# First attention of a two-layer kernel: the eight products of a unit in one block, and the values, turns and unloads after them

## The chip, the cores and the metric

The kernel runs on one NeuronCore of a Trainium2 chip. The metric is the device time of one execution in microseconds (us), lower is better. PE is the matrix engine (TensorE), DVE the vector engine, ACT the scalar engine, POOL the GpSimd engine, SP the queue that issues most DMAs. PSUM is the memory that PE writes into; a "bank" below is one PSUM buffer of 128 partitions by 512 floats, and the kernel has eight of them.

## The reference, cut to what matters

Four batches of 1,024 tokens with 256 features go through two layers: attention, feed-forward, attention, and a mixture of experts, each with a residual and a layer norm. All is float32. The change touches the first attention, which has 16 heads of 16 dimensions:

```python
qkv = jnp.einsum('bsc,oc->bso', x, w_qkv).reshape(B, S, 3, H, D)
q = layer_norm(qkv[:, :, 0], q_gamma, q_beta)
k = layer_norm(qkv[:, :, 1], k_gamma, k_beta)
v = qkv[:, :, 2]
q, k = apply_rope(q, k)
attn = jnp.einsum('bqhd,bkhd->bhqk', q * D ** (-0.5), k)
attn = jax.nn.softmax(attn, axis=-1)
out = jnp.einsum('bhqk,bkhd->bqhd', attn, v).reshape(B, S, C)
out = jnp.einsum('bsc,oc->bso', out, w_proj) + b_proj
```

## The kernel before, in words

**Groups and units.** The 16 heads of a batch are worked on in four groups of four heads, so there are sixteen groups in all, numbered n = 4b + g. Each group goes over its 8 x 2 blocks of scores (128 by 512) twice. The first pass (class `Maxima`, `head`, line 467) makes the scores with queries on the partitions, and DVE reduces each to its row maxima (line 470). The second pass (class `Attend`, `head`, line 491) makes the scores again with keys on the partitions and the maximum folded in as a seventeenth dimension, and ACT takes the exponential (line 500). `values` (line 509) then multiplies the exponentials with the values. Both products have only up to 32 rows to contract over, and each of the four heads lies in its own 32 partitions, so they are "row-tile" products: four of them can run in the array at once. The value products write 32 partitions each and are "column-tile" products. Everything else on PE (projections, transposes, feed-forward) uses the whole array.

**The unit.** `first_units(b)` (from line 1047) runs the second pass of group n together with the first pass of group n+1. For each of 16 steps i it puts out a unit: four score products of group n (`at.head`), four of group n+1 (`mx.head`), and the values of step i-1. A float32 product is two rows of the profile, so the eight products are sixteen rows. Before the change they stand in two blocks of four products. The values stand between the two blocks, and so does, in some steps, one of these: a `turn` (line 458: four transposes that make queries or keys feature-major, copied out by ACT, line 461; at i = 3, 10 and 12 to 15) or an `unload` (line 524: four transposes of the attention's output, read out by DVE, lines 527 and 528; at i = 5 for the last group, and at i = 11). The last group of the last batch has no group after it, so its units hold only four products.

**Banks.** The score products of both kinds take their banks in turn from one pool of six (`ps_s`, tag `s`). The values have one bank of their own (`ps_av`), and turns, unloads and all pieces of other work inside these units share the last one (`ps_m`, tag `m`, asked for with `bank(name, False)`, line 139). A product can start when the reader of the bank's last tile is done.

**What sets the order.** All this runs inside a hand-written schedule: the order in which the Python code puts instructions out is the order on each engine's queue. `weave` (line 1139) takes unit after unit and puts pieces of other stages (projections, feed-forward, routing) between them, about as many as there are units or fewer. At PE the queue is thus: block, values, turn or unload, block, piece, next unit. Work due later (`later`, `tick`) goes on DVE and POOL between units.

Of the kernel before, what the change touches and what calls it, by code (L numbers as in the profile page):

```python
# [35 lines left out]
def postln_layers_kernel(ctx: ExitStack, tc: tile.TileContext, a: dict, out: bass.AP):  # L36
# [74 lines left out]
    with ExitStack() as main:  # L111
# [932 lines left out]
        groups = {}  # L1044
        oq0, oT1, ends = {}, {}, {}

        def first_units(b):

            oq0[b] = act.tile([P, TB, C], F32, tag="oq", bufs=2, name=f"oq0_{b}")
            last = None  # L1050
            for g in range(G0):
                n = 4 * b + g
                at = Attend(groups[n], oq0[b])
                mx = groups.get(n + 1)
                for i in range(16):
                    for hp in range(2):

                        then = []
                        for j in range(2):
                            if mx is not None:  # L1060
                                then += [at.head(i, 2 * hp + j), mx.head(i, 2 * (1 - hp) + j)]
                            elif hp == 0:
                                then += [at.head(i, 2 * j), at.head(i, 2 * j + 1)]
                        for fn in then:
                            fn()
                        if hp == 0:
                            if i > 0:
                                at.values(i - 1)
                            elif last is not None:
                                last.values(15)  # L1070
                            if i == 3:
                                groups[n].turn(0, 1, name="a")
                            if i == 5 and last is not None:
                                last.unload(1)
                            if i == 10 and mx is not None:
                                mx.turn(0, 0, name="a")
                            if i == 11:
                                at.unload(0)
                            if i >= 12 and n + 2 in groups:
                                groups[n + 2].turn((i - 12) // 2, i % 2)  # L1080
                    if i == 0:
                        groups[n].close(1)
                    if i == 3 and n + 2 < G0 * B:
                        nb, ng = divmod(n + 2, G0)
                        groups[n + 2] = Maxima(nb, ng)
                    if i >= 4 and n + 2 in groups:
                        groups[n + 2].rotate(4)
                    if i == 8 and mx is not None:
                        mx.close(0)
                    yield  # L1090
                last = at
            last.values(15)

            def end(big):
                last.unload(1, big)

            ends[b] = end
# [206 lines left out]
        def second_end(b):  # L1304
# [4 lines left out]
        cut = 19  # L1309
        weave(  # L1310
            first_units(0), 64, early + stash, False, [lambda big: load_heads(1, 0)], 30, [f for f in prep if f], 0
        )
        flush()
        load_ahead()
        load_heads(1, 1)
        for t in range(TB):
            load_x(1, t)
        weave(first_units(1), 64, project_v(1) + first_end(0) + ffn0(0) + project1(0), False, [lambda big: load_heads(2, 0)], 30)
        for b in (1, 2):
            ffn = ffn0(b)  # L1320
            ends_b = first_end(b)
            weave(
                second_units(b - 1),
                29,
                ends_b[:1] + load_v(b + 1) + [lambda big, b=b: load_heads(b + 1, 1)] + ends_b[1:] + ffn[:cut],
                True,
            )
            weave(
                first_units(b + 1),
                64,  # L1330
                second_end(b - 1) + ffn[cut:] + project1(b),
                False,
                [lambda big, b=b: load_heads(b + 2, 0)] if b + 2 < B else (),
                30,
                dispatch(b - 1, False),
                30,
            )
# [261 lines left out]
```

## Time and profile before

| what | value |
|---|---|
| three runs | 2453.25, 2458.11, 2460.34 us; median 2458.11 us |
| the profiled execution | 2456.11 us |
| its span, first to last instruction | 2454.4 us (1.7 us lie around it) |
| mean granted PE clock | 0.958 |
| stretches with units of the first attention | 71.8 to 703.0, 864.5 to 1186.3, 1349.1 to 1647.9 us |
| granted clock from 71.8 to 364.2, 364.2 to 703.0, 864.5 to 1186.3, 1349.1 to 1589.6 us | 1.00, 1.00, 0.99, 1.00 |
| PE, DVE, ACT, POOL busy in the span | 2317.0, 1385.0, 1018.4, 741.7 us |

The page of the profile counts an engine's busy time, then follows the chain of work that ended last back through the span. The groups add up all instructions of one line. The timeline lists single instructions in order of time; `xN` at a line's end means that N of them were merged, and square brackets give the engine's idle time before the instruction and what ended it. The ends of matmuls in it are modelled, so that rows of PE overlap and a PE that waits for less than the pipeline's length still counts as busy. What a step of PE costs is therefore read from start to start: from its first row to the first row of the next step. `32*128` means that a product contracts over 32 rows (row tile), `128*32` that it writes 32 columns (column tile), `128*128` the whole array.

### The profile page before, as it was taken

How to read it: one execution, taken by the hardware profiler on the slowest of the kernel's cores; microseconds unless marked ns; L12 is line 12 of the kernel's file. 1: busy time of each engine (PE TensorE's matmuls, PEld its weight loads, DVE VectorE, ACT ScalarE, POOL GpSimd, SP SyncE). 2: the span in 40 equal slices, each digit the busy share in tenths (PEclk: the TensorE clock that was granted, in tenths of full speed). 3: DMA queues.
4: the chain of work that ended last, by engine and by line, in shares of the span. 5: the costliest groups of instructions: out<-in, count | busy, mean ns of one | idle time of the engine just before them, and what ended most of it. 6: DMA issues, size and time to landing. Idle time of an engine off the chain costs nothing.

```text
span 2454.4 us, 36158 instructions
## 1 busy us (share of the span) xinstructions
PE 2317.0 (94%) x14004; PEld 1150.6 (47%) x14004; DVE 1385.0 (56%) x3227; ACT 1018.4 (41%) x2037; POOL 741.7 (30%) x1101
## 2 busy tenths in 40 slices
PE   8999999999999999999999999999999974999994
PEld 5333334444444543444445434445566432666662
DVE  7766666666557376785573867716635673111113
ACT  2565655555543445545333554562332231111112
POOL 5335337223214144262241420301111153222223
PEclk9999999999989999999899999998999786999997
DMA  3233120000000000010000000111000011444444
GB/s 102 61 128 132 55 78 29 18 11 1 1 28 1 1 1 23 1 65 15 32 1 1 1 1 10 61 44 57 1 1 1 1 66 57 112 112 106 105 88 148
DMA packets 78124, 107.77 MB, mean 44 GB/s; under 512 B 8832, under 2 KB 67200, under 8 KB 76288
## 3 DMA queue, kind: packets, MB, share of 16 engines
q1 hardware_dynamic: 48592, 73.34, 9.1%
q0 software_dynamic: 9984, 14.82, 3.2%
q10 hardware_dynamic: 19376, 17.30, 2.3%
q8 instruction: 110, 1.80, 0.3%
q14 instruction: 62, 0.51, 0.1%
HBM read 66.54 MB, written 38.90 MB: 43 GB/s over the span
## 4 chain that ended last, share of the span: by engine, by line
PE 87%; DVE 8%; DMA 1%; POOL 1%; issue 1%; ACT 1%; SPq 0%; DVEq 0%; POOLq 0%; ACTq 0%
PE sc L491 20%; PE av L509 10%; PE ph L1460 7%; PE gu L655 7%; PE py L1476 7%; PE sc L981 5%; PE mx L931 4%; PE mx L467 4%; PE p L900 4%; PE dn L671 4%; PE av L1018 3%; PE dn L1018 2%; DVE masked L941 2%; PE ppa L589 2%; PE qk L320 2%; PE pt L458 1%
## 5 line engine op out<-in xcount | busy, mean ns | idle before, releaser
L470 DVE TENSOR_REDUCE part<-mx 128x1 f32<-128x512 f32 x1024 | 655.9, 684 | 304.9 <-PE mx L467 299.3
L500 ACT ACTIVATE pe<-sc 128x512 f32<-128x512 f32 x1024 | 554.1, 596 | 397.3 <-PE mx L467 344.3
L467 PE MATMUL mx<-kT,qT 32*128 32x512 f32 x2048 | 630.5, 638 | 2.1 <-DVE part L470 1.9
L491 PE MATMUL sc<-qT,kT 32*128 32x512 f32 x2048 | 605.6, 638 | 0.0
L491 PEld LDWEIGHTS sc<-qT,kT 32*128 32x128 f32 x2048 | 176.4, 183 | 219.5 <-issue 175.8
L509 PE MATMUL av<-pe,va 128*32 128x512 f32 x2048 | 273.8, 606 | 0.0
L992 ACT ACTIVATE pe<-sc 128x512 f32<-128x512 f32 (+3 forms) x384 | 157.3, 498 | 215.6 <-PE sc L981 215.3
L467 PEld LDWEIGHTS mx<-kT,qT 32*128 32x128 f32 x2048 | 189.2, 183 | 40.2 <-DVE part L470 21.2
L941 DVE CUSTOM_DVE_ANT_0 masked<-mx,mask_w 128x128 bf16<-128x128 f32 (+3 forms) x256 | 125.5, 490 | 121.2 <-PE mx L931 89.5
L1460 PE MATMUL ph<-dmT,f 128*128 128x512 f32 x384 | 170.2, 602 | 4.4 <-DVE dmT L99 3.5
L1468 ACT ACTIVATE hTm<-ph,b 128x512 f32<-128x512 f32 x96 | 60.7, 683 | 261.3 <-PE ph L1460 261.3
L1476 PE MATMUL py<-f,hTm 128*128 128x256 f32 x768 | 167.7, 379 | 0.0
L995 POOL TENSOR_SCALAR_AFFINE_SELECT pe<-pe 128x256 f32<-128x256 f32 x128 | 53.8, 429 | 369.6 <-ACT pe L992 368.0
L1480 POOL DMA_INDIRECT acc_d<-yo,dm x48 | 74.7, 1555 | 285.1 <-DVE yo L1478 243.6
L1476 PEld LDWEIGHTS py<-f,hTm 128*128 128x128 f32 x768 | 146.2, 190 | 24.7 <-issue 5.7
L931 PE MATMUL mx<-kT,qT 32*128 32x512 f32 (+3 forms) x768 | 144.0, 603 | 4.1 <-DVE x L556 3.2
L385 POOL TENSOR_TENSOR ss<-ss,neg_half 128x16 f32<-128x16 f32 x48 | 139.1, 2906 | 0.5
L1477 DVE TENSOR_TENSOR yo<-py,b 128x256 f32<-128x256 f32 x48 | 20.4, 425 | 207.2 <-PE py L1476 207.2
L981 PE MATMUL sc<-qT,kT 32*128 32x512 f32 (+3 forms) x768 | 131.7, 577 | 3.6 <-DVE part L941 2.0
L509 PEld LDWEIGHTS av<-pe,va 128*32 128x32 f32 x2048 | 40.5, 108 | 192.4 <-issue 186.2
L1460 PEld LDWEIGHTS ph<-dmT,f 128*128 128x128 f32 x384 | 72.9, 192 | 94.7 <-issue 86.6
L655 PE MATMUL gu<-xTf,wg 128*128 128x256 f32 x384 | 107.3, 402 | 0.3 <-ACT pe L992 0.3
(346 smaller groups left out, 2955.6 us busy)
## 6 DMA issues: line engine op xcount, KB each, us to landing
f<-in_fc SPq DMA_DIRECT2D x14, 1024.0 KB, 5.0
f<-in_fc ACTq DMA_DIRECT2D x10, 1024.0 KB, 6.3
disp_d<-empty ACTq DMA_DIRECT2D x12, 520.0 KB, 3.4
xink<-in_xT SPq DMA_DIRECT2D x24, 256.0 KB, 2.9
qk_d<-xs SPq DMA_DIRECT2D x6, 1024.0 KB, 5.1
xr<-qk_d SPq DMA_DIRECT2D x6, 1024.0 KB, 7.1
dm<-disp_d SPq DMA_DIRECT2D x11, 520.0 KB, 3.7
x<-in_x SPq DMA_DIRECT2D x32, 128.0 KB, 2.8
```

The source lines that it names most:

```text
L467: nc.tensor.matmul(sc, self.qT[r, t * P : (t + 1) * P], self.kT[r, u * 512 : (u + 1) * 512], start=True, stop=True)
L470: return lambda: nc.vector.tensor_reduce(self.part[:, t, u, h : h + 1], sc, AX.X, ALU.max, negate=True)
L491: nc.tensor.matmul(sc, self.m.kT[r, kt * P : (kt + 1) * P], self.m.qT[r, qb * 512 : (qb + 1) * 512], start=True, stop=True)
L500: nc.scalar.activation(self.pes[i, h // 2][:, h % 2, :], sc, AF.Exp)
L509: nc.tensor.matmul(self.av[32 * h : 32 * h + 32, :], va0[:, kt, 4 * self.g + h, :], self.pes[i, h // 2][:, h % 2, :], start=kt == 0, stop= ...
L655: nc.tensor.matmul(ps[:, i * 256 : (i + 1) * 256], w[:, c, f * P : (f + 1) * P], xT[j][:, c, :], start=c == 0, stop=c == 1,)
L931: nc.tensor.matmul(scs[h][:, :n], qT[r, t * P : (t + 1) * P], kT[r, u * 512 : u * 512 + n], start=True, stop=True,)
L941: nc.vector.tensor_tensor_reduce(masked[:, :n], scs[h][:, :n], mask_w[:, 512 - n :], -1.0, -NEG, ALU.add, ALU.min, part)
L981: nc.tensor.matmul(scs[h][:, off:], ones_h[r, :] if w else kT[r, kt * P : (kt + 1) * P], (self.m.nmT if w else qT)[r, q], start=w == 0, st ...
L992: nc.scalar.activation(pe[:, j, off:], scs[2 * hp + j][:, off:], AF.Exp)
L1460: nc.tensor.matmul(ph[:, i * CAP : (i + 1) * CAP], f1[:, c, (f + i) * P : (f + i + 1) * P], dmT[:, c, :], start=c == 0, stop=c == 1,)
L1476: nc.tensor.matmul(py[:, :C], hT[:, f, c * P : (c + 1) * P], f2[:, f, :], start=f == 0, stop=f == FF1 // P - 1)
```

## The change

Inside a unit the loop over two halves (`hp`) is gone. The four heads' products of both groups are put out one after the other, eight products in one block; behind them come the values of the step before, and then the turn or unload of the step. The pairs of heads stay the same (`at` head h with `mx` head h+2 modulo 4), and so does the order of products, exponentials and maxima. Number, shape and buffers of all instructions stay the same. On PE the queue of a unit becomes: block of eight, values, turn or unload, piece. On ACT the copy of a turn stands behind four exponentials, where it stood behind two; on DVE the two reads of an unload stand behind four maxima, where they stood behind two. POOL and SP keep their order. In the last group, which has no `mx`, the order of instructions stays as it was.

```diff
                 for i in range(16):
-                    for hp in range(2):
-
-                        then = []
-                        for j in range(2):
-                            if mx is not None:
-                                then += [at.head(i, 2 * hp + j), mx.head(i, 2 * (1 - hp) + j)]
-                            elif hp == 0:
-                                then += [at.head(i, 2 * j), at.head(i, 2 * j + 1)]
+
+                    for h in range(4):
+                        then = [at.head(i, h)]
+                        if mx is not None:
+                            then.append(mx.head(i, (h + 2) % 4))
                         for fn in then:
                             fn()
-                        if hp == 0:
-                            if i > 0:
-                                at.values(i - 1)
-                            elif last is not None:
-                                last.values(15)
-                            if i == 3:
-                                groups[n].turn(0, 1, name="a")
-                            if i == 5 and last is not None:
-                                last.unload(1)
-                            if i == 10 and mx is not None:
-                                mx.turn(0, 0, name="a")
-                            if i == 11:
-                                at.unload(0)
-                            if i >= 12 and n + 2 in groups:
-                                groups[n + 2].turn((i - 12) // 2, i % 2)
+                    if i > 0:
+                        at.values(i - 1)
+                    elif last is not None:
+                        last.values(15)
+                    if i == 3:
+                        groups[n].turn(0, 1, name="a")
+                    if i == 5 and last is not None:
+                        last.unload(1)
+                    if i == 10 and mx is not None:
+                        mx.turn(0, 0, name="a")
+                    if i == 11:
+                        at.unload(0)
+                    if i >= 12 and n + 2 in groups:
+                        groups[n + 2].turn((i - 12) // 2, i % 2)
```

## The prediction

> **What bounds the kernel now.** I read the page first, for the bound, then the timeline of PE through the units of the first attention, then the two places in it where the trace already shows what the change makes of every unit.
>
> ```profile
> PE 2317.0 (94%) x14004; PEld 1150.6 (47%) x14004; DVE 1385.0 (56%) x3227; ACT 1018.4 (41%) x2037; POOL 741.7 (30%) x1101
> ...
> PE 87%; DVE 8%; DMA 1%; POOL 1%; issue 1%; ACT 1%; SPq 0%; DVEq 0%; POOLq 0%; ACTq 0%
> ...
> L470 DVE TENSOR_REDUCE part<-mx 128x1 f32<-128x512 f32 x1024 | 655.9, 684 | 304.9 <-PE mx L467 299.3
> L500 ACT ACTIVATE pe<-sc 128x512 f32<-128x512 f32 x1024 | 554.1, 596 | 397.3 <-PE mx L467 344.3
> ```
>
> PE carries the chain (87%). The two readers of the score banks wait for PE and not the other way round: DVE idles 304.9 us before its maxima, ACT 397.3 us before its exponentials. So time on PE in these units is time of the kernel. An ordinary unit with a piece (PE rows of the timeline; one row of each step left in, each block has eight):
>
> ```profile
> 447.38 0.69 PE L491 MATMUL sc<-qT,kT 32*128 32x512 f32 x1
> ...
> 447.91 0.59 PE L491 MATMUL sc<-qT,kT 32*128 32x512 f32 x1
> ...
> 448.45 1.07 PE L509 MATMUL av<-pe,va 128*32 128x512 f32 x8
> 449.44 0.69 PE L491 MATMUL sc<-qT,kT 32*128 32x512 f32 x1
> ...
> 450.51 1.13 PE L655 MATMUL gu<-xTf,wg 128*128 128x256 f32 x4
> ...
> 452.44 0.69 PE L491 MATMUL sc<-qT,kT 32*128 32x512 f32 x1
> ```
>
> From start to start: block 1.07 us, values 0.99, block 1.07, piece 1.93. No gap: PE sets the pace. The second block costs no wait although it needs two banks that the first one filled (eight products, six banks): the values give ACT and DVE 0.99 us to empty them.
>
> **What sixteen rows in one block cost.** Where no piece stands between two units, the second block of one and the first of the next already touch. The trace has 47 such long blocks: 46 of 3.00 to 3.01 us and one of 4.93. One of the 46 (rows of PE, ACT and DVE, in order of time):
>
> ```profile
> 280.86 0.69 PE L491 MATMUL sc<-qT,kT 32*128 32x512 f32 x1
> ...
> 282.02 1.57 ACT L500 ACTIVATE pe<-sc 128x512 f32<-128x512 f32 x3 [0.47 <-PE mx L467]
> 282.06 1.29 DVE L470 TENSOR_REDUCE part<-mx 128x1 f32<-128x512 f32 x2 [1.36 <-PE mx L467]
> ...
> 282.26 1.10 PE L491 MATMUL sc<-qT,kT 32*128 32x512 f32 x2
> 282.81 0.69 PE L467 MATMUL mx<-kT,qT 32*128 32x512 f32 x1
> ...
> 283.86 1.07 PE L509 MATMUL av<-pe,va 128*32 128x512 f32 x8
> ```
>
> The first four products run together; the next two take the last free banks; the seventh and eighth cannot start before the first exponential and the first maximum, which begin at 1.16 and 1.20 us, are done. They start at 1.87 and 1.95 us (282.81 is the eighth) and the block ends at 3.00. Apart from each other, two blocks cost 2 x 1.07 = 2.14. So one block of sixteen rows costs 3.00 - 2.14 = **+0.86 us**.
>
> A rule of the Trainium skill speaks for the change: "TensorEngine Tiling (Array Packing)", section Tiling Modes, says that changing the tiling mode drains the engine, and the change makes each unit change mode less often. The rows bear the drain out: at the edges of a block a pass of four takes 0.53 us, and inside the long block the second pass gives way after 0.43 (0.53 to 0.96). By the drain alone one long block would take 4 x 0.43 + 2 x 0.10 = 1.92 us and save 0.22 in a unit, 190 x 0.22 = 42 us in all (the 190 comes below). By the row it takes 3.00, this saving already in it. The row decides, because it holds the bank wait too.
>
> **The change part by part.** I went through PE's timeline unit by unit. 240 of the 256 units have eight products; the last 16 have four and keep their order, cost nothing.
>
> *Units without a piece* cost nothing: their 3.00 us seam between units is taken away and put inside a unit, with the values now at the seam. *Units with a piece*: 52, 62, 45 and 31 in batches 0 to 3, together 190 (a unit that had no values between its blocks, at the start of a batch, is left out). There 2.14 becomes 3.00: 190 x 0.86 = **+163 us**. Nothing covers it; the values that covered it now come after the wait.
>
> Corrections of that, from the same timeline. Where the piece is a gate and up product (48 units), DVE's two operations on it let the maxima start 1.32 us after the block's start (448.70 against 447.38) rather than 1.20, which the values hid: 48 x 0.12 = +6. In about 28 units DVE's or another engine's work delays the second block already, to 1.8 us or more; there the delay stays, the values no longer lie in it, and the cost is a whole 1.00 rather than 0.86: 28 x 0.14 = +4. In 23 units that follow a short piece (0.59 us of transposes) the first block takes 1.34, not 1.07, since it waits for the banks of the block just before; the values will stand in between: 23 x 0.27 = -6. Together **+4 us**.
>
> *Turns and unloads move* from between the blocks to just ahead of the piece. They write the bank `m`, and so does every piece in these units; with the one bank, the piece has to wait for the copy out. Before, the second block (1.07 us) lay in between and hid this. The last group, with no second block, shows it uncovered, a turn first, then an unload (PE, ACT and DVE rows):
>
> ```profile
> 1598.31 0.66 PE L458 MATMUL pt_1a<-ident,tokq 128*128 128x128 f32 x4
> 1599.38 0.62 ACT L461 COPY qT<-pt_1a 128x512 f32<-128x512 f32 x1
> 1600.06 1.13 PE L900 MATMUL p<-xTa,w1q 128*128 128x256 f32 x4 [1.09 <-ACT qT L461]
> ...
> 1606.38 0.66 PE L524 MATMUL pto<-ident,avs 128*128 128x128 f32 x4
> 1607.08 0.26 DVE L527 RECIPROCAL rc<-pto 128x16 f32<-128x16 f32 x1 [19.96 <-PE pto L524]
> 1607.37 0.42 DVE L528 TENSOR_TENSOR oq<-pto,rc 128x256 f32<-128x256 f32 x1
> ```
>
> The unload's piece starts at 1607.94, 1.56 us after the unload; the four transposes themselves take 0.59, so the wait is 0.97. DVE is free then as it will be after the change: the fourth maximum ends near 3.0 + 0.1 + 0.7 = 3.8 us of a unit, the unload at 3.00 + 1.00 + 0.59 = 4.59. The turn's copy begins late in this row because ACT still has exponentials (1.07 us). After the change they end near 3.6, a full microsecond before the turn does, so I take the delay of a turn with a free ACT: in the unit at 280.27 the copy begins 0.70 after the transposes (280.97), takes 0.58, and 0.06 more pass before the piece as in the row above: 1.34 - 0.59 = 0.75. Bounds: 0 if something hid it, 1.16 if ACT were as late as in the row shown (1.75 - 0.59). 92 of the 190 units have both a turn or unload and a piece: 69 turns x 0.75 = 52 and 23 unloads x 0.97 = 22, **+74 us**. A turn without a piece behind it is followed by a long block, which needs other banks, and costs nothing.
>
> What queues behind the new waits: behind the seventh product on PE stand the eighth, the values and the piece; ACT and DVE get the last two tiles later, but wait for PE anyway. The exponentials are needed by the values of the next unit only, after its long block. The later copy of a turn is first read in the next unit or later. POOL's and SP's queues keep their order, and longer units only give their transfers more room: nothing, or a few us less of the present waits.
>
> Sum: 163 + 4 + 74 = +241 us, on the profiled execution's 2456.1 (span 2454.4 and 1.7 around it): 2697. The median of the runs shown is 2.0 above that execution, so I say **2698 us**.
>
> **The rivals.**
> - *Only the bank wait*: if the copy of a turn or unload were hidden after all, 163 + 4 remain: 2625. The rows of the last group speak against it. 8%.
> - *A deeper backlog*: the wait for the first maximum passes every delay of DVE on to PE, with no values to absorb it; if this cost 0.25 us more in each of the 190 units, +48: 2746. Against it: 46 equal long blocks in the trace, in busy and quiet stretches. 8%.
> - *The drain counts and the banks don't*: a long block of 1.92 and the turn's waits, 2456 - 42 + 74 = 2488. Against it: those same 46. 2%.
> - *Not slower: emptying the banks is the bound already.* If four maxima and the work of a piece on DVE (4 x 0.64 + 0.84 = 3.4 us in the unit shown) set the unit's length, a wait on PE would lie inside it and the time would stay at 2458. It decides from the point where DVE's work exceeds PE's 5.06 us of that unit; it is 1.66 short, and DVE's 304.9 us of idling say the same. 2%.
>
> The forecast has 80%.
>
> **How the numbers follow.** Its own range: the long block between +0.83 and +1.00 in 190 units (158 to 190), the turns and unloads between 0.55 and 0.98 in 92 (51 to 90): 2456 + 209 to 2456 + 280, 2665 to 2736. I give 2655 to 2738, which reaches some way towards both slower-side rivals. Faster by over 0.3% (about what a measurement of this kernel can tell from no change): 1%; within it 2%; slower 97%.
>
> **What would show it.** In the profile after, PE's timeline should show blocks of sixteen rows of 3.0 us in nearly all 240 units, their last two products starting near 1.9 us; the wait of `mx` (L467) for `part` (L470) and of `sc` (L491) for `pe` (L500) should grow, by number more than by the idle time, as the modelled ends hide part of it. Pieces behind a turn should wait for `qT` or `kT` (L461), those behind an unload for `oq` (L528). A long block near 1.9 us would break the first step; pieces that start 0.59 us after a turn, the second. Second attention and experts should stay as long as they are.

## The result and the profile after

The changed kernel takes 2676.91 us (median of four runs, 2674.09 to 2679.78) against 2457.73 us before: a ratio of 1.091, 95% interval 1.088 to 1.095. The forecast was 2698 us, in a range of 2655 to 2738.

The page of the kernel after, lines of parts 1, 4 and 5:

```profile
PE 2479.7 (93%) x14004; PEld 1234.3 (46%) x14004; DVE 1386.5 (52%) x3227; ACT 1025.9 (38%) x2037; POOL 742.3 (28%) x1101
...
PE 87%; DVE 7%; ACT 2%; issue 1%; POOL 1%; DMA 1%; SPq 0%; DVEq 0%; POOLq 0%; ACTq 0%
...
L470 DVE TENSOR_REDUCE part<-mx 128x1 f32<-128x512 f32 x1024 | 656.3, 684 | 351.2 <-PE mx L467 346.8
L500 ACT ACTIVATE pe<-sc 128x512 f32<-128x512 f32 x1024 | 554.2, 598 | 343.7 <-PE mx L467 282.9
```

This page alone would mislead. PE does the same 14,004 rows and is "busy" 163 us longer: most of the new waiting lies inside the modelled length of matmuls and counts as work. The share of 93% says nothing about PE being well used. ACT has 2% of the chain now, where it had 1%: of its 60 us there, 43 are the copies of line 461 that pieces wait for. The waits show only from start to start. One unit with a gate and up piece after the change, from the timeline (PE, ACT and DVE; the unit is of the same kind as the one shown of before):

```profile
526.07 0.69 PE L491 MATMUL sc<-qT,kT 32*128 32x512 f32 x1
...
527.23 1.57 ACT L500 ACTIVATE pe<-sc 128x512 f32<-128x512 f32 x3 [0.67 <-PE mx L467]
527.39 2.58 DVE L470 TENSOR_REDUCE part<-mx 128x1 f32<-128x512 f32 x4
...
528.12 0.69 PE L467 MATMUL mx<-kT,qT 32*128 32x512 f32 x1
...
529.17 1.07 PE L509 MATMUL av<-pe,va 128*32 128x512 f32 x8
530.17 1.13 PE L655 MATMUL gu<-xTf,wg 128*128 128x256 f32 x4
...
532.09 0.69 PE L491 MATMUL sc<-qT,kT 32*128 32x512 f32 x1
```

The block lasts 3.10 us (529.17 - 526.07). Its eighth product starts at 528.12, 0.73 after DVE began the first maximum at 527.39. The four maxima take 2.58, so the first is done near 528.03, just before that product starts: its bank is what the product waits for. The unit takes 6.02 us where it took 5.06. Of the 240 units with eight products, 160 have a block of exactly 3.00, 49 one of 3.10 to 3.12 (48 units have a gate and up piece).

A turn and an unload, each with its piece, from the same timeline:

```profile
141.77 0.66 PE L458 MATMUL pt<-ident,tokq 128*128 128x128 f32 x4
142.47 0.59 ACT L461 COPY qT<-pt 128x512 f32<-128x512 f32 x1 [1.06 <-PE pt L458]
143.10 1.13 PE L320 MATMUL qk<-w,xink 128*128 128x256 f32 x4 [0.68 <-ACT qT L461]
...
186.47 0.66 PE L524 MATMUL pto<-ident,avs 128*128 128x128 f32 x4
187.17 0.26 DVE L527 RECIPROCAL rc<-pto 128x16 f32<-128x16 f32 x1 [0.89 <-PE pto L524]
...
188.03 1.10 PE L320 MATMUL qk<-w,xink 128*128 128x256 f32 x4 [0.90 <-DVE oq L528]
```

The pieces start 1.33 and 1.56 us after the turn and the unload, whose own transposes take 0.59. Brackets name whom they wait for: `qT` of line 461 and `oq` of line 528. The pieces shown read neither tile (their operands are `w` and `xink`), so what they wait for is the bank. ACT had waited 1.06 us for the turn, so its four exponentials were long done.

Both profiled executions, taken apart by walking PE's timeline from start to start over those 240 units (a part is good to about 1 us, by where the first and last unit of a batch is cut):

| part | before | after | difference | forecast |
|---|---|---|---|---|
| score blocks | 585.6 | 742.2 | +156.6 | +167 |
| turns and unloads with the waits behind them | 65.6 | 139.9 | +74.3 | +74 |
| values | 237.7 | 234.7 | -3.0 | 0 |
| pieces | 298.3 | 299.1 | +0.8 | 0 |
| everything outside these units | 1268.9 | 1263.9 | -5.0 | 0 |
| the profiled execution | 2456.11 | 2679.78 | +223.7 | +241 |

### The profile page after: what moved, and what is told of

Same layout as the page of the kernel before. It is cut to its first block, busy times and chain, and to the rows that moved or that the text cites. A ratio compares the mean times of both kernels' runs of the same rounds, so it can differ in the third digit from the quotient of the medians.

```text
span 2678.0 us, 35967 instructions
## 1 busy us (share of the span) xinstructions
PE 2479.7 (93%) x14004; PEld 1234.3 (46%) x14004; DVE 1386.5 (52%) x3227; ACT 1025.9 (38%) x2037; POOL 742.3 (28%) x1101
## 4 chain that ended last, share of the span: by engine, by line
PE 87%; DVE 7%; ACT 2%; issue 1%; POOL 1%; DMA 1%; SPq 0%; DVEq 0%; POOLq 0%; ACTq 0%
PE sc L491 17%; PE mx L467 11%; PE av L509 9%; PE gu L655 6%; PE ph L1456 6%; PE py L1472 6%; PE sc L981 4%; PE mx L931 4%; PE p L900 4%; PE dn L671 3%; PE av L1018 3%; PE dn L1018 2%; DVE masked L941 2%; PE qk L320 2%; PE ppa L589 2%
## 5 line engine op out<-in xcount | busy, mean ns | idle before, releaser
L467 PE MATMUL mx<-kT,qT 32*128 32x512 f32 x2048 | 758.3, 627 | 0.8 <-DVE part L470 0.8
L491 PE MATMUL sc<-qT,kT 32*128 32x512 f32 x2048 | 724.7, 627 | 0.3 <-ACT pe L500 0.3
L491 PEld LDWEIGHTS sc<-qT,kT 32*128 32x128 f32 x2048 | 238.5, 183 | 248.0 <-ACT pe L500 175.1
L467 PEld LDWEIGHTS mx<-kT,qT 32*128 32x128 f32 x2048 | 240.9, 183 | 130.5 <-issue 102.1
L665 DVE SCALAR_TENSOR_TENSOR sg<-sg,gu 128x256 f32<-128x256 f32 x96 | 39.9, 416 | 188.8 <-ACT sg L664 188.7
```

Source lines behind the costliest of these rows:

```text
L467: nc.tensor.matmul(sc, self.qT[r, t * P : (t + 1) * P], self.kT[r, u * 512 : (u + 1) * 512], start=True, stop=True)
L491: nc.tensor.matmul(sc, self.m.kT[r, kt * P : (kt + 1) * P], self.m.qT[r, qb * 512 : (qb + 1) * 512], start=True, stop=True)
```

## The experiments

The theory: the price is two single resources. A block of eight products runs into six score banks, which costs 0.86 us in a unit with a piece; and a piece behind a turn or unload waits for the one bank `m`. Rivals: a long block is slow in itself (modes, number of rows), and the waits behind turns come from the later places of the copies on ACT and DVE. "Before" in a ratio is the kernel before, run on the same chip as the version it stands beside.

**1. Turn ahead of the values.** One part of the change taken back: only the place of the turn or unload.

```diff
                         for fn in then:
                             fn()
+                    if i == 3:
+                        groups[n].turn(0, 1, name="a")
...
                     if i > 0:
                         at.values(i - 1)
                     elif last is not None:
                         last.values(15)
-                    if i == 3:
-                        groups[n].turn(0, 1, name="a")
...
```

> The changed kernel, with the turn or unload put between the block and the values instead of behind the values; all else as changed. Theory (one bank for turns and pieces): the values (1.00 us) now cover the copy of a turn (0.75) and the reads of an unload (0.97), so the 92 waits of the changed kernel, 74 us in its profile, go: about 2677 - 74 = 2603. The long blocks stay at 3.00. Rival (the waits come from the place of the copies on ACT and DVE, behind four exponentials or maxima, which stays as it is): the pieces go on waiting, nothing or little changes, 2660 or more.

Measured: 2602.59 us, ratio to before 1.0614 (1.0582 to 1.0645). On the timeline:

```profile
140.36 0.66 PE L458 MATMUL pt<-ident,tokq 128*128 128x128 f32 x4
...
140.94 1.07 PE L509 MATMUL av<-pe,va 128*32 128x512 f32 x8
141.05 0.59 ACT L461 COPY qT<-pt 128x512 f32<-128x512 f32 x1
141.94 1.13 PE L320 MATMUL qk<-w,xink 128*128 128x256 f32 x4
```

The copy (to 141.64) now lies under the values, and the piece starts with no wait. Turns and unloads cost 65.8 us over the 240 units, as before the change; the blocks 742.5, as after it. The copy still stands behind four exponentials, so its place there does not cause the waits of the changed kernel: the rival falls. What is left of the change, the long block alone, costs 6.1%.

**2. Turn ahead of the piece, blocks as before.** The other part alone.

```diff
                         if hp == 0:
                             if i > 0:
                                 at.values(i - 1)
...
-                            if i == 3:
-                                groups[n].turn(0, 1, name="a")
...
+                    if i == 3:
+                        groups[n].turn(0, 1, name="a")
...
                     if i == 0:
                         groups[n].close(1)
```

> The kernel before with one part of the change alone: its two blocks of four stay, values between them, but the turn or unload moves from between the blocks to just ahead of the piece. Theory: the piece waits for bank m, and longer than in the changed kernel, since the exponentials of the second block hold ACT until 4.3 us of the unit: about 1.2 us in 69 units with a turn and 1.5 in 23 with an unload, +118; in 20 units without a piece the turn now parts two blocks that touched, 3.00 becomes 1.07 + 1.34, -12. About 2458 + 106 = 2564. Rival (each wait as in the changed kernel, 0.75 and 0.97): 2458 + 74 - 12 = 2520. If the move of the turns costs nothing by itself: 2446.

Measured: 2550.11 us, ratio 1.041 (1.038 to 1.044).

```profile
134.97 0.66 PE L458 MATMUL pt<-ident,tokq 128*128 128x128 f32 x4
...
135.12 1.08 ACT L500 ACTIVATE pe<-sc 128x512 f32<-128x512 f32 x2 [0.98 <-PE mx L467]
136.09 0.59 ACT L461 COPY qT<-pt 128x512 f32<-128x512 f32 x1
136.73 1.13 PE L320 MATMUL qk<-w,xink 128*128 128x256 f32 x4 [1.11 <-ACT qT L461]
```

Here the copy does wait for exponentials, those of the second block (two from 135.12, 1.08 us), and the piece comes 1.76 us after the turn: a wait of 1.17 rather than 0.75. Turns and unloads take 114.0 us more than before (179.6 against 65.6; expected 118), the blocks 13.8 less (571.8; expected 12 less). The median rose by 97 us, where 106 was expected. So the move of the turns costs more by itself than in the change, where the values separate the turn from the exponentials. The two parts alone, 6.1 and 4.1%, come to more than the 9.1% of both.

**3 and 4. Six products, in two blocks and in one.** Both kernels leave out the first-pass products and maxima of two of the four heads of every group but the first (their maximum is taken as zero), so that six banks are enough. The first keeps the order of before. The second has the long block, with turns between block and values, as in run 1, so that no piece waits for bank `m`.

```diff
-                                then += [at.head(i, 2 * hp + j), mx.head(i, 2 * (1 - hp) + j)]
+                                then.append(at.head(i, 2 * hp + j))
+                                if hp == 0:
+                                    then.append(mx.head(i, 2 + j))
```

```diff
                     for h in range(4):
                         then = [at.head(i, h)]
-                        if mx is not None:
-                            then.append(mx.head(i, (h + 2) % 4))
-                        for fn in then:
-                            fn()
+                        if mx is not None and h < 2:
+                            then.append(mx.head(i, h + 2))
+                        if h < 2:
+                            for fn in then:
+                                fn()
+                        else:
+                            held += then
...
+                    for fn in held:
+                        fn()
+                    if i > 0:
+                        at.values(i - 1)
```

> The kernel before, leaving out the first-pass products and maxima of two of the four heads of each group (their maximum is taken as zero), so that a unit has six products, four ahead of the values and two behind. Six banks are enough for the six. It is the base for the next kernel. Blocks of 1.07 and about 1.05 us; the 49 seams without a piece shrink from 3.00 to about 1.91, since no bank is missing there: about 2458 - 53 - 15 = 2390.

> The same six products (the same two heads' maxima left out) in one block as the change has it, with turns put between block and values and their copies ahead of the last two exponentials, so that no piece waits for bank m. Theory (what a long block costs is the missing banks): no product waits, the block takes about 1.91 us against 1.07 + 1.05 in two, and the change pays: 190 x 0.21 = 40 us less than the six products in two blocks, about 2350. Rival (a long block is slow in itself, banks or not: +0.86 in each of 190 units, or part of that): slower than the two blocks, up to 2390 + 163 = 2553.

Measured: 2394.17 us in two blocks, ratio to before 0.975 (0.972 to 0.978), and 2342.40 in one, ratio 0.954 (0.951 to 0.957). The two intervals lie apart. First the timeline of the two blocks, then that of the one:

```profile
427.19 0.69 PE L493 MATMUL sc<-qT,kT 32*128 32x512 f32 x1
...
428.26 1.06 PE L511 MATMUL av<-pe,va 128*32 128x512 f32 x8
...
429.26 1.13 PE L493 MATMUL sc<-qT,kT 32*128 32x512 f32 x4
...
430.31 1.13 PE L657 MATMUL gu<-xTf,wg 128*128 128x256 f32 x4
```

```profile
414.53 0.69 PE L493 MATMUL sc<-qT,kT 32*128 32x512 f32 x1
...
416.46 1.06 PE L511 MATMUL av<-pe,va 128*32 128x512 f32 x8
417.46 1.13 PE L657 MATMUL gu<-xTf,wg 128*128 128x256 f32 x4
```

Blocks of 1.07 and 1.05 us against one of 1.93, which 225 of the 240 units have. With banks enough the same rearrangement pays: the blocks take 508.2 us in two and 471.5 in one, 36.7 less. So a long block is not slow in itself; this one has twelve rows, and run 5 keeps all sixteen. The other 15 of the 52 us between the two medians are mostly values that wait less (253.8 against 240.2).

**5. Five banks.** The changed kernel with one size changed.

```diff
-        ps_s = main.enter_context(tc.tile_pool(name="ps_s", bufs=6, space=PSUM))
+        ps_s = main.enter_context(tc.tile_pool(name="ps_s", bufs=5, space=PSUM))
```

> The changed kernel with five score banks in place of six, one size changed. Judged by the length of the long blocks in the first attention alone, since the second attention has the same pool and will be slower for its own reasons. Theory (the products wait for a bank's reader): the sixth product now needs the first exponential, the seventh the first maximum, the eighth the second exponential, half a microsecond after the first: it starts near 2.4 rather than 1.95 us, and the block takes about 3.4 us rather than 3.00. Rival (length set by the modes or by the number of rows in a block): 3.00 as before.

Measured in one execution: 206 of the 240 blocks take 3.40 or 3.41 us. The execution takes 2821.48; of the 142 us over the changed kernel's profiled execution about 90 are these blocks, and the rest lies outside these units.

```profile
118.33 0.69 PE L491 MATMUL sc<-qT,kT 32*128 32x512 f32 x1
...
119.53 1.29 DVE L470 TENSOR_REDUCE part<-mx 128x1 f32<-128x512 f32 x2 [2.35 <-PE mx L467]
119.55 1.57 ACT L500 ACTIVATE pe<-sc 128x512 f32<-128x512 f32 x3 [0.74 <-PE mx L467]
...
120.20 0.69 PE L467 MATMUL mx<-kT,qT 32*128 32x512 f32 x1
...
120.28 0.69 PE L491 MATMUL sc<-qT,kT 32*128 32x512 f32 x1
...
120.69 0.69 PE L467 MATMUL mx<-kT,qT 32*128 32x512 f32 x2
...
121.74 1.07 PE L509 MATMUL av<-pe,va 128*32 128x512 f32 x8
```

121.74 - 118.33 is 3.41. The sixth product starts at 120.20, the seventh at 120.28, and the eighth at 120.69, once the second exponential has emptied its bank. With the pair above this settles the banks as the cause of the long block's price. Seven or eight score banks for all eight products were not tried, nor a second bank `m`: six score banks, one for the values and one for the pieces make up the eight.

**6 and 7. A version that beats both.** If touching blocks are the trouble, the kernel before has it too, at its seams without a piece (3.00 rather than 2.14). In 20 of these units a turn or unload lies between the blocks, where the values already part them. Kernel 6 puts it at the seam there; `NO_PIECE` lists the 20 units, `moves` holds the six `if`s.

```diff
-                            if i == 3:
-                                groups[n].turn(0, 1, name="a")
...
+                            if 16 * n + i not in NO_PIECE:
+                                moves()
+                    if 16 * n + i in NO_PIECE:
+                        moves()
```

Kernel 7 moves turns and unloads by some units as well, so that 35 seams get one (`MOVED` holds their new steps):

```diff
+                            moves(i, DUE.items(), MOVED.get(n, {}))
+                    moves(i, MOVED.get(n, {}).items(), ())
```

> The kernel before, where in the 20 units that have a turn or unload but no piece behind them this goes from between the blocks to the end of the unit, so that it parts two blocks that touched. Theory (banks): there 3.00 becomes 1.07 + 1.34, as before after a short piece, 20 x 0.59 = 12 us less, 2446 against 2458, ratio 0.995. Rival (a seam costs nothing that a short filler can hide, or the copy of the turn comes up elsewhere): no change.

> The kernel before, where turns and unloads are also moved by a few units, so that 35 of the 46 seams without a piece get one. Theory (banks): 35 x 0.59 = 21 us less than before, ratio 0.9915, faster than both kernels and than the version with 20. Rival: no change, or slower, if the moved turns wait for tokens or for the shared bank.

Measured: kernel 6 takes 2435.47 us, ratio 0.990 (0.988 to 0.991); kernel 7 takes 2436.24, ratio 0.991 (0.989 to 0.993). Both are about 1% faster than the kernel before, and neither beats the other, where kernel 7 was expected to lead. Kernel 6's blocks take 12.1 us less than before (573.5), as worked out. Its profiled execution gained 14.8, about 3 of them in the second attention of the last batch, which the edit does not touch; its median gained 24. That further gain comes with a higher granted clock: 0.963 and 0.964 in three of its four runs and 0.959 in the profiled one, against 0.956 to 0.957 in all seven runs of before. What raised the clock is not shown, so 12 us is what the version itself is shown to give. Kernel 7 gained 23 (granted clock 0.959 to 0.961), near the 21 expected, but its blocks only 15.2 (570.4). In its trace 32 of 36 parted seams take 2.41 us together; the other four take longer, and for what is not shown.

## Why the prediction was right, point by point

*PE sets the pace of these units.* Right: the whole took 223.7 us more, nearly all that PE's steps in the units lost (+228.7). The rival in which emptying the banks was the bound already is out. The sum itself is 1 us short: 2456.1 + 241 + 2.0 is 2699, not 2698.

*One block of sixteen rows costs 3.00, +0.86 in 190 units.* Right, read from 46 cases in the trace of before: 160 blocks at 3.00. Its cause is shown by runs 3 to 5.

*Corrections, +4.* Half right. Gate and up pieces stretch the block to 3.10 to 3.12, as worked out. The 23 short-piece waits went. The assumption that failed is "in about 28 units DVE's or another engine's work delays the second block already ... there the delay stays": the blocks came out at +156.6, not +167. It rests in part on a misreading. The trace of before has 28 such second blocks, but only 17 take 1.79 us or more; the other 11 take 1.16 to 1.59. And most of the delay did not stay: before, the 28 exceeded 1.07 us by 19.4 us in all, and after the change the blocks of the same units exceed 3.00 by 8.8. That the longer units gave the late engine time is an argument, not tested. One of the 28 was a piece waiting 1.73 us for a DMA (`xinv`, line 297, in the unit at 370.60 of before); the unit fell from 6.83 to 5.92 us with the wait gone.

There were errors the other way too. Twelve blocks came out at 3.88, all in units right behind an output projection (line 589), whose residual DVE adds first. Six of these had a second block of 1.81 or more before and did keep their delay, at a cost of 0.60 to 1.00 each. Two had one of 1.22 to 1.23 and cost about 1.6. Four have no piece of their own and had been counted at nothing. "A few us less of the present waits" was said, with no number put in the sum; that term was undersized by about 10 us net, with 2 or 3 more in the values. The nearness of the total is thus partly errors that offset each other.

*Turns and unloads, +74.* Right, wait by wait: 69 waits of 0.74 to 0.75 and 23 of 0.92 to 0.97. Taking the turn's delay from a row with a free ACT, and not from the row in which the piece was seen to wait (1.16), was the choice that mattered; run 2 shows what the other gives, 1.17.

*The drain.* The rule of the Trainium skill that changing the tiling mode drains the engine ("TensorEngine Tiling (Array Packing)", section Tiling Modes) agrees with the rows of runs 3 and 4: 0.22 us a unit and 42 us in all by the prediction's estimate, 0.19 and 36.7 measured. In the changed kernel the short inner pass is there too (526.61 to 527.04 in the unit shown, 0.43 us), and the wait for banks outweighs it.

*Outside.* The remaining 5.0 us of the difference lie after the last unit of the first attention, almost all in the second attention of the last batch (423 us before, 418 after, with a granted clock of 0.87 and 0.88). The change does not touch it; why the clock differs is not shown.

## What to carry to other kernels

Before you put like products in one block to save changes of mode, count the banks against the products of a block: with a bank for each, the longer block paid here (six products on six banks, 1.93 us against 2.12); past that, products waited for a reader (eight on six, 3.00 against 2.14). Work between two blocks that looks like an interruption may be the cover under which banks empty; ask of every step you move what its copy-out was hidden by, and what uses its bank next. And read PE from start to start: its busy share went only from 94% to 93% while the time grew by 9%.

## What the runs showed of the hardware

Two row-tile products alone take as long as four at once: 1.05 against 1.07 us (run 3). So a block whose last products start only as a pair loses the concurrency of the tiles, not just the wait: in the unit at 280.86 of before, the seventh and eighth start 1.87 and 1.95 us after the block's start, and the block still runs to 3.00. With five banks the sixth, seventh and eighth products come one by one as banks are read out (120.20, 120.28 and 120.69 in the unit shown, 1.87, 1.95 and 2.36 us after its start), and the block grows by another 0.41 us.
